# Selective scan: the last block of the convolution moved from the front into four steps of the scan

## The chip, the cores and the metric

The kernel runs on one core of a Trainium2 chip. Its time is device time in microseconds (us), the median of several executions of the whole program. The engines are PE (matrix multiply), DVE (vector), ACT (activation functions), POOL (the second elementwise engine) and SP, which here only issues transfers. Each engine works through its own list of instructions in order and waits on semaphores for the others.

## The reference, cut to what matters

Eight images of 64 x 64 positions and 96 channels go through four layers. Layers 0 and 2 are selective scans over 192 inner channels and a state of 16; layer 1 is a chunked scan, layer 3 a spectral layer. Cut to a selective scan:

```python
xm, z = split(einsum('bhwc,ec->bhwe', x, in_proj_w))
xc = silu(depthwise_conv3x3(xm) + conv_b)          # this change is about this line
xs = [xc by rows, xc by columns, both reversed]    # four directions
dts, Bs, Cs = split(x_proj_weight @ xs)
delta = softplus(dt_projs @ dts + bias)
h = h * exp(delta * A) + (delta * u) * B           # a scan over 4096 positions
y = sum over the state of h * C, plus u * D
```

The four directions are then added, normalised, gated by `silu(z)` and projected back. Everything is in float32.

## The kernel before

One image is worked on at a time, layer after layer, so there are 16 selective scans in the program (8 images, layers 0 and 2). `project` leaves the projected input in `y` (96 partitions, two halves of 192 channels, 4096 positions). `selective_scan` makes the convolution with its silu from `y` into `u`, and then runs 32 steps: four directions `k` of eight chunks of 512 positions.

**The front.** The 64 rows are cut into eight blocks of eight rows (512 positions). `conv` makes blocks 0 to 4 on DVE, tap by tap (lines 254 and 256). `conv_block` makes blocks 5, 6 and 7 on PE: nine taps for each half, each a matmul (line 267) of `y`, shifted, with a diagonal matrix of that tap's weights, summed in PSUM. The 18 diagonals are made by POOL (`diagonals`, line 261) into a buffer of the tile `c`. `silu` (line 270) on ACT adds the bias and writes `u`. Between these calls the inputs of steps 0 and 1 are prepared by `prepare_part`. PSUM buffers of the front (`p_conv`) are given back before the two buffers `da` of the steps are taken; DVE's memsets of `da` (line 674) are thus the first thing that waits for the front's last silu.

**A step** has six groups `n` of 32 channels and four states of each partition row. For each group:

- `spread` (line 541, PE) copies a group's `du` over the 128 partitions into the PSUM tile `pu`, which has one buffer.
- `with_b` (line 547) multiplies by B into `db`: on DVE, reading `pu`, for groups 0, 1, 3 and 4; on POOL for groups 2 and 5.
- `decays` (line 562, ACT) makes the exponentials into `da[0]` and `da[1]`, two instructions each.
- `scan` (line 577, DVE) runs twice, once per `da`, into `h`, of which there are five buffers.
- `leave` copies the last state (line 593, ACT) and multiplies `h` by C in place (line 598, POOL). `enter` (line 533, ACT) puts states into the `db` of a later group.
- `total_y` (lines 605 and 615, PE) sums three groups into `py`, which ACT copies to `y` (line 702). `py`, the two `pv` of `prepare` and nothing else share one PSUM buffer (the tag `py` of the pool `p_y`).

The order of all this is written out by hand: a loop over `t = 6 * i + n` (step `i`, group `n`) emits the calls, and each engine runs its instructions in the order of emission. At `n` = 2 the calls are, in order: first half scan of the group, exponentials ahead, second half scan, `leave`, `enter`, exponentials ahead, `with_b` of the next group. At `n` = 3 follow `spread` of group 4 and `total_y` of the first half. `prepare` makes the inputs of later steps in seven parts; its softplus (line 488) needs another activation table than the exponentials, so ACT loads a table before and after it. Block 7 of `u` is first read by the preparation of step 7, in step 5.

Of the kernel before, what the change touches and what calls it, by code (L numbers as in the profile page):

```python
# [9 lines left out]
F32 = mybir.dt.float32  # L10
AF = mybir.ActivationFunctionType
# [6 lines left out]
DM = 96  # L18
# [4 lines left out]
LC = 512  # L23
# [12 lines left out]
C_CW = C_OUT + 192  # L36
C_CB = C_CW + 18
# [27 lines left out]
def tile_vision_stack(  # L65
# [19 lines left out]
    nc = tc.nc  # L85
# [21 lines left out]
    ident = cst[:, K_ID : K_ID + 128]  # L107
# [34 lines left out]
    with (  # L142
# [6 lines left out]
        for i, (dtw, dtx, w) in enumerate(((dt0, dx0, w0s), (dt2, dx2, w2s))):  # L149
# [10 lines left out]
            for k in range(K):  # L160
                pw = pp.tile([DM, 2, 192], F32, name="pw", bufs=2)
                for hf in range(2):
# [4 lines left out]
                        start=True,  # L167
                        stop=True,
# [68 lines left out]
    def taps(y, rows, hf, acc):  # L237

        at, end = rows
        av = acc.rearrange("p (r c) -> p r c", c=64)  # L240
        xv = y[:, hf, :].rearrange("p (r c) -> p r c", c=64)
        for tap in (4, 0, 1, 2, 3, 5, 6, 7, 8):
            dy, dx = tap // 3 - 1, tap % 3 - 1
            r0, r1 = max(at, -dy), min(end, 64 - dy)
            c0, c1 = max(0, -dx), min(64, 64 - dx)
            src = xv[:, r0 + dy : r1 + dy, c0 + dx : c1 + dx]
            yield tap, src, av[:, r0 - at : r1 - at, c0:c1]

    def conv(w, y, u, rows, hf):
        out = u[:, hf, rows[0] * 64 : rows[1] * 64]  # L250
        for tap, src, dst in taps(y, rows, hf, out):
            cw = w[:, C_CW + hf * 9 + tap : C_CW + hf * 9 + tap + 1]
            if tap == 4:
                nc.vector.tensor_scalar_mul(dst, src, cw)
            else:
                nc.vector.scalar_tensor_tensor(dst, src, cw, dst, ALU.mult, ALU.add)
        silu(w, u, rows, hf, out)
# [7 lines left out]
    def conv_pe(dg, y, j, hf, acc):  # L265
        for tap, src, dst in taps(y, (8 * j, 8 * j + 8), hf, acc):
            nc.tensor.matmul(dst, dg[:, 9 * hf + tap, :], src, start=(tap == 4), stop=(tap == 8))

    def silu(w, u, rows, hf, acc):
        nc.scalar.activation(  # L270
            u[:, hf, rows[0] * 64 : rows[1] * 64],
            acc,
            AF.Silu,
            bias=w[:, C_CB + hf : C_CB + hf + 1],
        )
# [119 lines left out]
    def view(t, wh, at, n):  # L395

        if not wh:
            return t[:, at : at + n]
        return t.rearrange("p (h w) -> p w h", w=64)[:, at // 64 : (at + n) // 64, :]

    def cut(t, wh):

        return t.rearrange("p (w h) -> p w h", h=64) if wh else t

    def selective_scan(w, wdt, a, d, u, y):
# [23 lines left out]
        with (  # L429
# [86 lines left out]
            def groups(t):  # L516

                return t[:, 1:].rearrange("p (g s) -> p g s", s=SEG)[:, :, :LC]
# [67 lines left out]
            def leave(t, more):  # L586
# [10 lines left out]
                    prepare_part(i + 1)  # L597
                nc.gpsimd.tensor_mul(h, h, made[i]["c"])  # L598

            def total_y(i, hf):  # L600

                k, c = steps[i]
                wh = k % 2 == 1
                py = pyp.tile([128, LC], F32, name="py", tag="py")[:DM]
                nc.tensor.matmul(  # L605
                    py,
                    skip[:, hf, :] if k == 0 else ident[:DM, :DM],
                    view((u if k == 0 else y)[:, hf, :], wh, c * LC, LC),
                    start=True,
                    stop=False,  # L610
                )
                hs = [groups(made[i].pop(("h", 3 * hf + q))) for q in range(3)]
                for g in range(NSG):
                    for q in range(3):
                        nc.tensor.matmul(  # L615
                            py[32 * q : 32 * q + 32, :],
                            red,
                            hs[q][:, g, :],
                            start=False,
                            stop=(g == NSG - 1),  # L620
                        )
                return view(y[:, hf, :], wh, c * LC, LC), cut(py, wh)
# [3 lines left out]
            def prepare_part(i):  # L626
                if i < len(steps):
                    if i not in going:
                        going[i] = prepare(i)
                    next(going[i], None)  # L630
# [9 lines left out]
            with tc.tile_pool(name="p_conv", bufs=2, space=PSUM) as pvp:  # L640

                def conv_block(n):
                    acc = pvp.tile([DM, 2, LC], F32, name="acc")
                    for hf in range(2):
                        conv_pe(dg, y, n, hf, acc[:, hf, :])
                    return n, acc

                def silu_block(n, acc):
                    for hf in range(2):
                        silu(w, u, (8 * n, 8 * n + 8), hf, acc[:, hf, :])  # L650

                for hf in range(2):
                    conv(w, y, u, (0, 8), hf)
                for _ in range(5):
                    prepare_part(0)
                blocks = [conv_block(5)]
                conv(w, y, u, (8, 24), 0)
                for _ in range(2):
                    prepare_part(0)
                conv(w, y, u, (8, 24), 1)  # L660
                for _ in range(2):
                    prepare_part(1)
                blocks.append(conv_block(6))
                silu_block(*blocks[0])
                conv(w, y, u, (24, 40), 0)
                blocks.append(conv_block(7))
                silu_block(*blocks[1])
                conv(w, y, u, (24, 40), 1)
                silu_block(*blocks[2])
            with tc.tile_pool(name="p_da", bufs=1, space=PSUM) as pap:  # L670
                das = [pap.tile([128, 2 * SEG + 1], F32, name=f"da{p}") for p in range(2)]
                for da in das:
                    for at in range(3):
                        nc.vector.memset(da[:, at * SEG : at * SEG + 1], 0.0)
                states = {}
                for t in range(3):
                    enter(t)
                spread(0)
                decays(0, 0)
                decays(0, 1)  # L680
                with_b(0)
                for t in range(total + 2):
                    n, i = t % units, t // units
                    ahead = t + 1 < total
                    if n in (0, 3) and ahead:
                        spread(t + 1)
                    elif n in (1, 4) and t + 2 < total:
                        spread(t + 2)
                    if n == 0 and i > 0:
                        sums = total_y(i - 1, 1)  # L690
                    elif n == 3:
                        sums = total_y(i, 0)
                    elif n == 4:
                        prepare_part(i + 2)
                    if t < total:
                        scan(t, 0)
                        if n % 3 == 0 and t + 2 < total:
                            with_b(t + 2)
                    if ahead:
                        decays(t + 1, 0)  # L700
                    if n % 3 == 1 and t > 1:
                        nc.scalar.copy(*sums)
                    elif n == 0:
                        prepare_part(i + 1)
                    elif n == 5:
                        prepare_part(i + 2)
                    if t < total:
                        scan(t, 1)
                        leave(t, n == 3)
                    if t + 3 < total:  # L710
                        enter(t + 3)
                    if ahead:
                        decays(t + 1, 1)
                        if (n + 1) % 3 != 2:
                            with_b(t + 1)
                    if n in (0, 1, 5):
                        prepare_part(i + 1)

    def chunked_scan(w, d, u, y):

# [476 lines left out]
    for b in range(batch):  # L1197
        xd = xp.tile([DM, L], F32, name="xd")
        layers = (
            (w0s, lambda u, y: selective_scan(w0s, wdts[0], a0s, dsum[0], u, y)),  # L1200
            (w1s, lambda u, y: chunked_scan(w1s, dsum[1], u, y)),
            (w2s, lambda u, y: selective_scan(w2s, wdts[1], a2s, dsum[2], u, y)),
        )
        with tc.tile_pool(name="layers", bufs=1) as uyp:
            u = uyp.tile([DM, 2, L], F32, name="u")
            y = uyp.tile([DM, 2, L], F32, name="y")
            stats = uyp.tile([DM, 8, 6], F32, name="stats")
            sbs = [uyp.tile([DM, 2], F32, name=f"sb{n}") for n in range(3)] + [sb3]
            for n in range(4):
                with (  # L1210
# [3 lines left out]
                    if n == 0:  # L1214
                        xs = rp.tile([DM, L], F32, name="xs")
                        with (
# [3 lines left out]
                            src = x[b : b + 1].rearrange("b h w c -> (b h w) c")  # L1220
                            src = src.rearrange("(t p) c -> p t c", p=128)
# [21 lines left out]
        dst = out[b : b + 1].rearrange("b h w c -> (b h) w c").rearrange("h w c -> w h c")  # L1243
# [148 lines left out]
```

## Time and profile before

| | us |
|---|---|
| median of 3 runs | 29505.22 (29502.27 to 29553.22) |
| profiled execution, its own time | 29541.08 |
| its span | 29539.3 |
| DVE busy | 24797.7 (84%) |
| PE busy | 23139.1 (78%) |
| POOL busy | 21775.2 (74%) |
| ACT busy | 16410.5 (56%) |

Times in the trace count from the start of the span. An instruction's line gives its start, its length, its engine, its source line, the tile that it writes and those that it reads, and in brackets how long its engine had been idle before it and what ended that. The groups of the page give the number of instructions, their busy time in us and the mean length in ns, then the idle time ahead of them. A row of busy time by stretch gives the stretch, its length, the busy time of PE, PE's weight loads, DVE, ACT and POOL with the number of instructions, then PE's granted clock (1.00 is full speed), the share of the transfer engines and GB/s.

### The profile page before, as it was taken

The numbers are of one execution on the slowest core, as the hardware profiler recorded it, in microseconds if no ns is written. First come the engines' busy times: TensorE is split into PE (matmuls) and PEld (weight loads), VectorE is DVE, ScalarE is ACT, GpSimd is POOL, SyncE is SP. The second block draws the span as 40 slices with busy tenths as digits, with TensorE's granted clock in tenths as the row PEclk, the third lists the DMA queues.
The fourth block names the chain that finished last, engine by engine and source line by source line (L and its number), as shares of the span: only waits on it lengthen the run. The fifth ranks groups of instructions, "written<-read, shape, count | busy, mean of one in ns | idle before, by whom it ended". The sixth has DMA issues, their size and how long they took to land. (4 is left out here: it accounts for less than half of the span.)

```text
span 29539.3 us, 279023 instructions
## 1 busy us (share of the span) xinstructions
PE 23139.1 (78%) x89862; PEld 8801.1 (30%) x89862; DVE 24797.7 (84%) x17920; ACT 16410.5 (56%) x28541; POOL 21775.2 (74%) x8844
## 2 busy tenths in 40 slices
PE   7797877978779787797877978779787797877978
PEld 1151411514115142151421514215141151412414
DVE  9979699796897968979689796897979979699796
ACT  5546455464554645546455464554655546455564
POOL 8859488594885958859588495884958859587594
PEclk7787777877778777787777877778777787777877
DMA  5415254152541525415254152541525415254152
GB/s 124 103 38 133 66 122 102 39 133 65 121 103 39 132 67 120 104 39 131 67 118 105 38 132 68 118 105 38 132 68 122 102 38 132 67 122 102 43 131 65
DMA packets 1509730, 2727.51 MB, mean 92 GB/s; under 512 B 306584, under 2 KB 314104, under 8 KB 1503664
## 3 DMA queue, kind: packets, MB, share of 16 engines
q1 hardware_dynamic: 1491632, 2703.38, 39.2%
q8 instruction: 720, 11.80, 0.2%
q10 hardware_dynamic: 16640, 6.29, 0.1%
q14 instruction: 738, 6.05, 0.1%
HBM read 2325.26 MB, written 383.45 MB: 92 GB/s over the span
## 5 line engine op out<-in xcount | busy, mean ns | idle before, releaser
L577 DVE TENSOR_TENSOR_SCAN h<-da,db 128x1026 f32<-128x1026 f32 x6144 | 13728.7, 2280 | 505.4 <-PE py L615 170.7
L598 POOL TENSOR_TENSOR h<-h,c 128x2048 f32<-128x2048 f32 x3072 | 12749.2, 4178 | 143.2 <-ACT state L593 140.8
L541 PE MATMUL pu<-du,cst 32*128 32x512 f32 x4096 | 3238.8, 881 | 3528.1 <-DVE db L547 3493.8
L562 ACT ACTIVATE da<-dx,a0s 128x512 f32<-128x512 f32 x6144 | 4235.0, 690 | 2593.9 <-DVE h L577 2431.0
L562 ACT ACTIVATE da<-dx,a2s 128x512 f32<-128x512 f32 x6144 | 4234.9, 690 | 2593.2 <-DVE h L577 2428.1
L615 PE MATMUL py<-h,cst 128*32 128x512 f32 x24576 | 5404.1, 810 | 66.4 <-POOL h L598 66.4
L547 POOL TENSOR_TENSOR db<-du,b 128x2048 f32<-128x2048 f32 x1024 | 4653.5, 4544 | 583.9 <-ACT db L533 583.9
L547 DVE TENSOR_TENSOR db<-pu,b 128x2048 f32<-128x2048 f32 x2048 | 4637.5, 2264 | 6.7 <-issue 6.7
L615 PEld LDWEIGHTS py<-h,cst 128*32 128x32 f32 x24576 | 1177.9, 144 | 4956.0 <-issue 4505.2
L541 PEld LDWEIGHTS pu<-du,cst 32*128 32x128 f32 x4096 | 801.6, 243 | 5545.6 <-DVE db L547 4001.4
L463 PE MATMUL pv<-u,wk 96*128 96x512 f32 x2048 | 1766.6, 1004 | 751.1 <-ACT raw L459 751.1
L227 POOL TENSOR_SCALAR xn<-xs,sb 96x512 f32<-96x512 f32 x192 | 217.1, 1136 | 2773.4 <-DVE sb L207 2642.4
L454 PE MATMUL pv<-u,wk 96*96 96x512 f32 x2048 | 1486.2, 855 | 522.0 <-ACT state L593 252.1
L605 PE MATMUL py<-y,cst 96*96 96x512 f32 x1536 | 1551.3, 1108 | 400.5 <-ACT raw L468 361.6
L960 ACT ACTIVATE sg<-sg 128x768 f32<-128x768 f32 x1024 | 819.4, 800 | 1407.4 <-PE sg L944 1407.4
L506 POOL TENSOR_TENSOR du<-raw,u 96x512 f32<-96x512 f32 x1024 | 1443.9, 1434 | 0.0
L992 DVE TENSOR_TENSOR wt<-wt,cbm 128x768 f32<-128x768 f32 x1024 | 1022.3, 1004 | 496.6 <-ACT wt L961 496.4
L593 ACT COPY state<-h 128x4 f32<-128x4 f32 x3072 | 604.5, 197 | 1164.6 <-DVE h L577 1164.6
L1154 DVE SCALAR_TENSOR_TENSOR f<-p,w3bs,f 128x512 f32<-128x512 f32 x768 | 576.4, 750 | 719.6 <-ACT f L1147 692.8
L914 POOL TENSOR_TENSOR ce<-ec,cr 96x512 f32<-96x512 f32 x256 | 406.5, 1588 | 975.5 <-ACT ec L912 971.1
L891 POOL TENSOR_TENSOR rr<-lr,cc 128x768 f32<-128x768 f32 x256 | 375.9, 1468 | 1001.6 <-ACT lr L889 822.8
L463 PEld LDWEIGHTS pv<-u,wk 96*128 96x128 f32 x2048 | 534.3, 289 | 1910.2 <-ACT raw L459 1435.1
(207 smaller groups left out, 31983.9 us busy)
## 6 DMA issues: line engine op xcount, KB each, us to landing
dx<-dd SPq DMA_DIRECT2D x4096, 192.0 KB
b<-bcd SPq DMA_DIRECT2D x2048, 256.0 KB
c<-bcd SPq DMA_DIRECT2D x2048, 256.0 KB
du<-dud SPq DMA_DIRECT2D x2048, 128.0 KB
dd<-raw SPq DMA_DIRECT2D x1024, 192.0 KB
dud<-du SPq DMA_DIRECT2D x512, 128.0 KB
xd<-xs SPq DMA_DIRECT2D x256, 192.0 KB
xs<-xd SPq DMA_DIRECT2D x128, 384.0 KB
```

The source lines that it names most:

```text
L454: nc.tensor.matmul(pv[:DM], weights[k][:, hi, 128:], uv[hi], start=(hi == 0), stop=(hi == 1))
L463: nc.tensor.matmul(pv, weights[k][:, hi, :128], uv[hi], start=(hi == 0), stop=(hi == 1))
L506: nc.gpsimd.tensor_mul(cut(du[:, hf, :], wh), cut(delta[hf], wh), uv[hf])
L541: nc.tensor.matmul(pu, sel[rows, :], m["du"][rows, n // 3, :], start=True, stop=True)
L547: (nc.gpsimd if pool else nc.vector).tensor_mul(groups(m["db", n]), (m["du2"][:, n // 3, :] if pool else m["pu"]) .unsqueeze(1) .to_broadc ...
L562: nc.scalar.activation(dst[:, g, :LC], made[i]["dx"][n // 3][:, n % 3, :], AF.Exp, scale=av4[:, k, n, gs : gs + 1],)
L577: nc.vector.tensor_tensor_scan(made[i]["h", n][:, at][:, way], das[p][:, rev : 2 * SEG + rev][:, way], made[i]["db", n][:, at][:, way], 0. ...
L598: nc.gpsimd.tensor_mul(h, h, made[i]["c"])
L605: nc.tensor.matmul(py, skip[:, hf, :] if k == 0 else ident[:DM, :DM], view((u if k == 0 else y)[:, hf, :], wh, c * LC, LC), start=True, st ...
L615: nc.tensor.matmul(py[32 * q : 32 * q + 32, :], red, hs[q][:, g, :], start=False, stop=(g == NSG - 1),)
L960: nc.scalar.activation(sg, sg, AF.Abs)
L992: nc.vector.tensor_mul(it["wt"], it["wt"], m["cbm"][:, j : j + 1, :].to_broadcast([128, RK, Q]),)
```

## The change

Blocks 5 and 6 stay in the front. Block 7 is taken out of it, matmuls and silus, and made in four pieces, one at the end of group 2 of each of steps 1 to 4: half 0 in the first two, half 1 in the other two. The first piece of a half makes taps 4, 0, 1, 2 and 3; ACT copies the sum from PSUM to `u`. The second piece brings that back into PSUM with an identity matmul and adds taps 5 to 8. The diagonals are made anew for each piece by ACT, from the identity, with the tap's weight as the scale. After the fourth piece both halves get their silu in place. The accumulator takes the shared PSUM buffer `py`.

```diff
+            def conv_piece(n, piece):
+                hf, second = piece // 2, piece % 2 == 1
+                acc = pyp.tile([128, LC], F32, name="acc", tag="py")[:DM]
+                out = u[:, hf, n * LC : n * LC + LC]
+                if second:
+                    nc.tensor.matmul(acc, ident[:DM, :DM], out, start=True, stop=False)
+                mine = list(taps(y, (8 * n, 8 * n + 8), hf, acc))
+                mine = mine[5:] if second else mine[:5]
+                some = tp.tile([DM, 5, DM], F32, name="some")
+                for at, (tap, _, _) in enumerate(mine):
+                    col = C_CW + 9 * hf + tap
+                    nc.scalar.activation(
+                        some[:, at, :], ident[:DM, :DM], AF.Copy, scale=w[:, col : col + 1]
+                    )
+                for at, (tap, src, dst) in enumerate(mine):
+                    nc.tensor.matmul(
+                        dst, some[:, at, :], src,
+                        start=(tap == 4), stop=(at == len(mine) - 1),
+                    )
+                nc.scalar.copy(out, acc)
+                if piece == 3:
+                    for hf in range(2):
+                        at = slice(n * LC, n * LC + LC)
+                        nc.scalar.activation(
+                            u[:, hf, at], u[:, hf, at], AF.Silu,
+                            bias=w[:, C_CB + hf : C_CB + hf + 1],
+                        )
...
                 conv(w, y, u, (24, 40), 0)
-                blocks.append(conv_block(7))
                 silu_block(*blocks[1])
                 conv(w, y, u, (24, 40), 1)
-                silu_block(*blocks[2])
+            late = {(1 + n, 2): (7, n) for n in range(4)}
...
                     if n in (0, 1, 5):
                         prepare_part(i + 1)
+                    if (i, n) in late:
+                        conv_piece(*late[i, n])
```

More of the change, by code (lines that the diff above doesn't have):

```diff
@@ L598, in leave @@
                 nc.gpsimd.tensor_mul(h, h, made[i]["c"])
+            def conv_piece(n, piece):
[14 more added lines that the diff above has]
+                    nc.tensor.matmul(
+                        dst,
+                        some[:, at, :],
+                        src,
+                        start=(tap == 4),
+                        stop=(at == len(mine) - 1),
+                    )
[4 more added lines that the diff above has]
+                        nc.scalar.activation(
+                            u[:, hf, at],
+                            u[:, hf, at],
+                            AF.Silu,
+                            bias=w[:, C_CB + hf : C_CB + hf + 1],
+                        )
             def total_y(i, hf):
```

## The prediction

> **What bounds the kernel now.** First the page: no engine is at its peak, DVE has the most work, and the two groups that cost most belong to the selective scan, one on DVE and one on POOL.
>
> ```profile
> PE 23139.1 (78%) x89862; PEld 8801.1 (30%) x89862; DVE 24797.7 (84%) x17920; ACT 16410.5 (56%) x28541; POOL 21775.2 (74%) x8844
> ...
> L577 DVE TENSOR_TENSOR_SCAN h<-da,db 128x1026 f32<-128x1026 f32 x6144 | 13728.7, 2280 | 505.4 <-PE py L615 170.7
> L598 POOL TENSOR_TENSOR h<-h,c 128x2048 f32<-128x2048 f32 x3072 | 12749.2, 4178 | 143.2 <-ACT state L593 140.8
> ```
>
> These shares are averages over four layers, so I next asked for busy time in one stretch of one selective scan (four of its 32 steps). POOL is busy for 144.13 of 144.60 us and DVE for 141.13; a step takes 36.24 us. Both are full: a microsecond lost by DVE inside the steps is soon lost by POOL too, because each `h` has to be scanned before POOL multiplies it.
>
> ```profile
> 272.40:417.00 144.60, 107.05 (x272) 25.01 (x272) 141.13 (x65) 93.75 (x175) 144.13 (x41) 0.69 0.56 131
> ```
>
> Then the stretch ahead of the first step, engine by engine. DVE ends its share of the convolution at 103.5 us and stands still for 22.49 us. It waits for the last `silu` (L270) on ACT, and that waits for PE, which makes blocks 6 and 7 in one run of 72 passes from 92.86 (an fp32 matmul is two passes).
>
> ```profile
> 125.95 0.62 DVE L674 MEMSET da<- 128x1 f32 x6 [22.49 <-ACT u L270]
> ...
> 92.86 31.72 PE L267 MATMUL acc<-y,c 96*96 96x512 f32 x72
> ...
> 109.97 1.26 ACT L270 ACTIVATE u<-acc,w0s 96x512 f32<-96x512 f32 x2 [16.48 <-PE acc L267]
> 111.12 1.14 ACT L270 ACTIVATE u<-u,w0s 96x1024 f32<-96x1024 f32 x1
> 124.62 1.26 ACT L270 ACTIVATE u<-acc,w0s 96x512 f32<-96x512 f32 x2 [12.36 <-PE acc L267]
> 125.78 0.38 ACT L533 COPY db<-zero 128x4 f32<-128x4 f32 x3
> ```
>
> Last, the place in a step where the pieces will stand. I take step 4 and count from T0 = 290.73 us, where DVE's scans of group 2 end.
>
> ```profile
> 290.73 2.26 DVE L547 TENSOR_TENSOR db<-pu,b 128x2048 f32<-128x2048 f32 x1
> ...
> 291.05 1.41 ACT L562 ACTIVATE da<-dx,a0s 128x512 f32<-128x512 f32 x2
> 293.05 2.07 PE L541 MATMUL pu<-du,cst 32*128 32x512 f32 x2 [5.97 <-DVE db L547]
> ...
> 295.43 1.42 ACT L562 ACTIVATE da<-dx,a0s 128x512 f32<-128x512 f32 x2 [2.97 <-DVE h L577]
> ...
> 297.50 2.26 DVE L547 TENSOR_TENSOR db<-pu,b 128x2048 f32<-128x2048 f32 x1
> ...
> 299.86 4.48 DVE L577 TENSOR_TENSOR_SCAN h<-da,db 128x1026 f32<-128x1026 f32 x2
> ```
>
> PE has stood idle for 5.97 us before L541, and that matmul of two passes takes 2.07 us, where the same one at 302.48 takes 1.12. So PE is cold here. In all 16 selective scans the L541 at this place takes 2.07 us in steps 1 to 4, after 5.8 to 6.7 us of idleness.
>
> [...] Granted clock (third number from the right), with PE busy first after the length:
>
> ```profile
> 3768.85:3772.26 3.41, 0.00 (x0) 0.00 (x0) 3.34 (x3) 0.00 (x0) 3.41 (x4) 1.00 0.58 173
> 3772.26:3775.67 3.41, 2.65 (x3) 0.95 (x4) 3.23 (x4) 0.00 (x0) 3.41 (x4) 0.50 1.00 227
> 3775.67:3779.08 3.41, 3.41 (x6) 1.14 (x5) 3.34 (x4) 1.15 (x1) 3.41 (x3) 0.50 1.06 217
> 3779.08:3782.50 3.42, 3.42 (x10) 1.34 (x9) 3.35 (x3) 0.00 (x0) 3.42 (x3) 1.00 0.32 61
> ```
>
> An empty window turns PE cold; convolution taps begin at 3773.02 and PE is warm only after the first window filled from end to end, 6.06 us later. In three other dense runs it took 6.0, 5.3 and 3.7 us. [...] here the next ACTIVATE follows the 1.28 us load at once, so I use the trace.
>
> **The change part by part, per selective scan** (16 of them: 8 images, 2 layers).
>
> *Removed from the front.* 36 passes of block 7 (14.66 us from 109.92 to 124.58, all on the path) and their two silus. ACT's copies at L533, the last thing before the first exponentials, then follow the silu that ends at 112.26 instead of the one that ends at 125.88. **Gain 13.6 us.** DVE is done by then, and all transfers for step 0 have landed by about 100 us. In the 16 scans DVE's wait at L674 is 17.75 to 22.5 us, so the gain fits everywhere.
>
> *Added to steps 1 to 4.* The built program's order on DVE, POOL and SP is unchanged, and no DMA is added. ACT gets, after the L562 that ends at T0+1.73, five (or four) 96x96 activations for the diagonals [...], and then the copy of `acc`, at which it stands until PE is done. PE gets the taps between two L541: the one for group 3 and the one for group 4 that DVE needs at T0+6.77. That is the crux: L541 today ends 2.4 us ahead of its reader.
>
> - First tap: T0+1.73 and one diagonal: T0+2.1 (2.0 to 2.6). Later diagonals hide behind taps.
> - Tap cost: block 7 shows 0.84 ns per element and pass warm, twice that cold. Pieces 0 and 2 stream 2536 elements twice: 4.25 us warm. Pieces 1 and 3 stream 1834 behind the first diagonal: 3.07 us; their identity matmul runs earlier, in PE's idle time.
> - With a cold time C a piece takes its warm time + C/2. [...] So 6.8 and 5.6 us, and 0.13 for the last pass to land.
> - Pieces 0 and 2 end at T0+9.03. L541 then takes 1.0, a semaphore 0.05, and DVE's L547 for group 4 starts at T0+10.08 instead of T0+6.77: **3.3 us late**. ACT's copy (0.58) and exponentials end at T0+11.1, ahead of the scan (T0+12.4), so they cost nothing.
> - Piece 1 ends at T0+7.85: **2.1 us late**.
> - Piece 3 also has two silus with a table load on each side, as the Softplus pair has at L488 (3.94 us in all). ACT: 7.85 + 0.05 + 0.58 + 3.94 + 1.41 + 0.05 = T0+13.9 for the exponentials that the scan needs at T0+9.13: **4.75 us late**.
>
> What waits behind that: group 3's state copy on ACT and POOL's product for it move by at most 2.5 us and are caught up within the step, since DVE stays later; `py` of L615 starts later but on a warm PE, done 2 us before the scan of group 5 that reuses its `h`. DVE and POOL are both full, so next to nothing is won back; I allow 0.3 us of slack in POOL.
>
> **Sum:** 13.6 + 0.3 - (2 x 3.3 + 2.1 + 4.75 = 13.5) = 0.4 us per scan, 6 us in all. The profiled execution took 29541.08 us, 0.12% over the median 29505.22; the difference is applied to the median: **29499 us**. A measurement of this kernel can tell about 0.2% (59 us, 3.7 us per scan) from no change.
>
> **Bounds.** C = 3.4 everywhere: stalls 2 x 2.46 + 1.28 + 3.9 = 10.1, a gain of 3.8 per scan, 29444 us. Taps cold to the end (8.5 and 6.15 us): stalls 2 x 5.0 + 2.66 + 5.28 = 17.95, a loss of 4.05, 29570 us.
>
> **Rivals.**
> - *PE doesn't stay cold* (0.10, faster). If the identity matmul or an odd phase keeps the clock up, the pieces take 4.25 and 3.07 us: stalls 2 x 0.76, 0 and 2.2, a gain of 10 per scan, 29345 us. Against it: 64 of 64 cold matmuls at this place.
> - *PE never warms inside a piece* (0.14, slower). Between 294.07 and 300.90 PE is busy throughout and only the second window counted. If diagonal waits or short taps make windows that don't count, it is the cold bound: 29570. It decides from stalls above 17.6 us per scan. Against it: runs of the same taps at 3773 warmed in their first full window.
> - *The front has another limit* (0.02, slower): with no gain at L674 only the stalls are left, 16 x 13.2, 29716 us. Against it: the chain above.
> - The balance: 0.74.
>
> From these: faster 0.13 (the first rival, and 0.03 of the balance's low end); slower 0.16 (0.10 of the second rival, which lies just past the bound, the third, and 0.04 of the balance's high end); same 0.71. The range, 29440 to 29572, reaches from bound to bound; the first and third rivals stay outside it.
>
> **What would show it.** DVE's idle time at the memset (328.3 us before) falls by 218. DVE's L547 waits for PE's L541 by about 175 us in all, L577 for ACT after piece 3 by about 42 more. The granted clock is 0.5 at each first tap. I am wrong if DVE's stall per piece averages below 2.4 or above 4.3 us, or if the scan starts less than 13 us earlier.

## Result and profile after

The changed kernel takes 29523.07 us (median of 20 runs) against 29518.53 us before (20 runs). The ratio is 1.0004, with a 95% interval of 0.9997 to 1.0011. A second comparison, further down, gave 1.0011 (1.0003 to 1.0018). That is no change by the 0.2% of the forecast, which was 29499 us, no change. The second interval lies just above 1, so a loss of about 0.1% or less is more likely than the gain of 6 us that was forecast; the sign is not settled.

Nothing here was hidden: two large edits cancel. The first place to look is DVE's list of waits in the trace of after. Its columns are the waiting instruction, what it waited for, the time in all, how often, and the longest.

```profile
DVE db L547 <- PE pu L541: 175.8, 64, 6.0
...
DVE h L577 <- ACT da L562: 147.2, 311, 2.7
...
DVE da L710 <- ACT u L270: 88.3, 16, 7.8
```

The same list of before has two of these waits:

```profile
DVE da L674 <- ACT u L270: 328.3, 16, 22.5
...
DVE h L577 <- ACT da L562: 98.8, 288, 0.7
```

The memset behind the front (L710, L674 before) waits 88.3 us in 16 scans, where it was 328.3. That is the gain, 240 us. The first line of after did not exist before: DVE waits 64 times, once per piece, for PE's L541. The wait for ACT's exponentials was 98.8 us, so 48.4 us are new. The two new waits make 224 us.

The same in the page's groups of after. POOL's product L598 now waits 321.8 us (143.2 before), nearly all of it for ACT's state copy L593, and DVE's L547 waits for PE.

```profile
L598 POOL TENSOR_TENSOR h<-h,c 128x2048 f32<-128x2048 f32 x3072 | 12746.6, 4177 | 321.8 <-ACT state L593 291.1
...
L547 DVE TENSOR_TENSOR db<-pu,b 128x2048 f32<-128x2048 f32 x2048 | 4637.8, 2265 | 183.8 <-PE pu L541 175.8
```

**The front** of the first scan, in the timelines of DVE, PE and ACT:

```profile
109.78 0.62 DVE L710 MEMSET da<- 128x1 f32 x6 [6.17 <-ACT u L270]
110.86 2.29 DVE L547 TENSOR_TENSOR db<-pu,b 128x2048 f32<-128x2048 f32 x1 [0.46 <-ACT db L533]
113.78 4.48 DVE L577 TENSOR_TENSOR_SCAN h<-da,db 128x1026 f32<-128x1026 f32 x2 [0.63 <-ACT da L562]
...
92.78 15.63 PE L267 MATMUL acc<-y,c 96*96 96x512 f32 x36
...
108.45 1.26 ACT L270 ACTIVATE u<-acc,w0s 96x512 f32<-96x512 f32 x2 [14.81 <-PE acc L267]
109.60 1.14 ACT L270 ACTIVATE u<-u,w0s 96x1024 f32<-96x1024 f32 x1
110.64 0.38 ACT L533 COPY db<-zero 128x4 f32<-128x4 f32 x3
```

PE makes 36 passes (two for each of 18 matmuls) instead of 72 and DVE waits 6.17 us instead of 22.49. The memsets now run beside ACT's last silu, so the first L547 gains a little more than the front and the first scan gives 0.63 us of it back.

**A piece.** Piece 0 of the same scan, all engines:

```profile
166.02 2.27 DVE L547 TENSOR_TENSOR db<-pu,b 128x2048 f32<-128x2048 f32 x1
...
167.68 1.43 ACT L612 ACTIVATE some<-cst,w0s 96x96 f32<-96x96 f32 x5
168.10 7.93 PE L616 MATMUL acc<-y,some 96*96 96x512 f32 x10 [6.30 <-ACT some L612]
...
175.96 1.12 PE L541 MATMUL pu<-du,cst 32*128 32x512 f32 x2
176.06 0.58 ACT L623 COPY u<-acc 96x512 f32<-96x512 f32 x1 [6.96 <-PE acc L616]
...
177.12 2.29 DVE L547 TENSOR_TENSOR db<-pu,b 128x2048 f32<-128x2048 f32 x1 [4.25 <-PE pu L541]
177.16 2.51 POOL L506 TENSOR_TENSOR du<-raw,u 96x512 f32<-96x512 f32 x2 [2.07 <-PE pu L541]
```

T0 is 166.02. The taps begin at T0+2.08 after 6.30 us in which PE stood still, and ten passes take 7.93 us; L541 for group 4, in line behind them, comes at T0+9.94, and DVE's L547 at T0+11.10 where it stood at T0+6.77. Then piece 3, where ACT is the later one:

```profile
287.20 5.24 PE L616 MATMUL acc<-y,some 96*96 96x504 f32 x8 [4.89 <-ACT some L612]
287.50 4.48 DVE L577 TENSOR_TENSOR_SCAN h<-da,db 128x1026 f32<-128x1026 f32 x2
...
293.07 1.28 ACT L627 ACT_TABLE_LOAD   x1
...
293.52 2.29 DVE L547 TENSOR_TENSOR db<-pu,b 128x2048 f32<-128x2048 f32 x1 [1.55 <-PE pu L541]
...
297.02 1.41 ACT L562 ACTIVATE da<-dx,a0s 128x512 f32<-128x512 f32 x2
...
298.37 0.18 ACT L593 COPY state<-h 128x4 f32<-128x4 f32 x1
...
298.46 8.85 DVE L577 TENSOR_TENSOR_SCAN h<-da,db 128x1026 f32<-128x1026 f32 x4 [2.65 <-ACT da L562]
...
298.63 4.17 POOL L598 TENSOR_TENSOR h<-h,c 128x2048 f32<-128x2048 f32 x1 [1.94 <-ACT state L593]
```

DVE first waits 1.55 us for PE, and 2.65 us more for exponentials that stand behind two silus and two table loads of 1.28 us. POOL's wait comes from the same queue: DVE has scanned group 3 by 291.98, but the state copy that POOL's product waits for stands on ACT behind all this and starts only at 298.37.

To see the balance per scan I took from both timelines the start of every L547 on DVE; means over the 16 scans:

| us | before | after | difference |
|---|---|---|---|
| first tap of the convolution to first L547 | 82.99 | 68.11 | -14.89 |
| step 0 | 36.28 | 36.77 | +0.49 |
| step 1 (piece 0) | 36.29 | 39.64 | +3.35 |
| step 2 (piece 1) | 36.42 | 38.88 | +2.46 |
| step 3 (piece 2) | 36.59 | 39.84 | +3.24 |
| step 4 (piece 3) | 36.33 | 41.42 | +5.09 |
| steps 5 to the last L547 | | | -0.04 |
| sum | 1240.64 | 1240.35 | -0.29 |

### The profile page after: what moved, and what is told of

Its sections match the earlier page's. It is cut to its first block, busy times and chain, and to the rows that moved or that the text cites. A ratio compares the mean times of both kernels' runs of the same rounds, so it can differ in the third digit from the quotient of the medians.

```text
span 29513.6 us, 279551 instructions
## 1 busy us (share of the span) xinstructions
PE 23206.7 (79%) x89926; PEld 8831.2 (30%) x89926; DVE 24808.5 (84%) x17920; ACT 16561.3 (56%) x28925; POOL 21765.8 (74%) x8844
## 5 line engine op out<-in xcount | busy, mean ns | idle before, releaser
L577 DVE TENSOR_TENSOR_SCAN h<-da,db 128x1026 f32<-128x1026 f32 x6144 | 13728.7, 2280 | 557.0 <-PE py L649 169.7
L598 POOL TENSOR_TENSOR h<-h,c 128x2048 f32<-128x2048 f32 x3072 | 12746.6, 4177 | 321.8 <-ACT state L593 291.1
L541 PE MATMUL pu<-du,cst 32*128 32x512 f32 x4096 | 3191.8, 869 | 3119.6 <-DVE db L547 3097.8
L649 PE MATMUL py<-h,cst 128*32 128x512 f32 x24576 | 5298.5, 796 | 61.2 <-POOL h L598 61.2
L547 POOL TENSOR_TENSOR db<-du,b 128x2048 f32<-128x2048 f32 x1024 | 4656.7, 4548 | 359.1 <-ACT db L533 359.1
L547 DVE TENSOR_TENSOR db<-pu,b 128x2048 f32<-128x2048 f32 x2048 | 4637.8, 2265 | 183.8 <-PE pu L541 175.8
L541 PEld LDWEIGHTS pu<-du,cst 32*128 32x128 f32 x4096 | 791.1, 240 | 5150.1 <-DVE db L547 3514.7
L506 POOL TENSOR_TENSOR du<-raw,u 96x512 f32<-96x512 f32 x1024 | 1446.5, 1438 | 41.5 <-PE pu L541 40.9
L593 ACT COPY state<-h 128x4 f32<-128x4 f32 x3072 | 603.7, 197 | 1114.0 <-DVE h L577 1113.9
```

Source lines behind the costliest of these rows:

```text
L506: nc.gpsimd.tensor_mul(cut(du[:, hf, :], wh), cut(delta[hf], wh), uv[hf])
L541: nc.tensor.matmul(pu, sel[rows, :], m["du"][rows, n // 3, :], start=True, stop=True)
L547: (nc.gpsimd if pool else nc.vector).tensor_mul(groups(m["db", n]), (m["du2"][:, n // 3, :] if pool else m["pu"]) .unsqueeze(1) .to_broadc ...
L577: nc.vector.tensor_tensor_scan(made[i]["h", n][:, at][:, way], das[p][:, rev : 2 * SEG + rev][:, way], made[i]["db", n][:, at][:, way], 0. ...
L649: nc.tensor.matmul(py[32 * q : 32 * q + 32, :], red, hs[q][:, g, :], start=False, stop=(g == NSG - 1),)
```

## Experiments

My theory: the front gives 14.4 us per scan, and four stalls take it back, because the taps stand on PE between two matmuls of a queue that DVE waits on, and begin while PE is cold. "Cold" means that the record of PE's granted clock has 0.50 there, "warm" that it has 1.00; in the traces of before and after it has no other value (a figure between them is a mean). Rivals: both edits are worth little; the length of a piece comes from the passes and the diagonals, not from the clock; or ACT's queue is what costs. Every ratio below is to the kernel before, timed on the same chip.

### One half of the change at a time

The front's half: block 7 leaves it, and one copy stands for the pieces.

```diff
-                    if (i, n) in late:
-                        conv_piece(*late[i, n])
+                    if (i, n) == (1, 2):
+                        nc.scalar.copy(u[:, :, 7 * LC :], y[:, :, 7 * LC :])
```

> Block 7 is taken out of the front and not made in pieces: the steps copy y to u there in one ACT instruction, so the convolution, bias and silu of block 7 are left out. Balance theory: the front gives 14.6 to 14.9 us per scan and nothing takes it back, so 235 us below the kernel before (about 0.8%, ratio 0.992). Rival (block 7 was hidden anyway, the two kernels are alike because both edits are worth little): ratio above 0.998.

Measured: 29297.9 us, ratio 0.9932 (0.9919 to 0.9944), 204 us less, 31 short of what was expected. DVE's wait at the memset is 91.1 us, and no wait for PE's L541 takes its place among DVE's waits but 1.4 us:

```profile
DVE h L577 <- ACT da L562: 106.9, 302, 0.6
DVE da L710 <- ACT u L270: 91.1, 16, 7.6
...
DVE h L577 <- PE pu L541: 1.4, 2, 0.7
```

The other half: the changed kernel with block 7 in the front as well.

```diff
                 conv(w, y, u, (24, 40), 0)
+                blocks.append(conv_block(7))
                 silu_block(*blocks[1])
                 conv(w, y, u, (24, 40), 1)
+                silu_block(*blocks[2])
```

> Block 7 is made twice: in the front as before, and again in the four pieces. Balance theory: the front is as long as before and steps 1 to 4 pay their stalls of about 14 us per scan, so 225 us above the kernel before (ratio 1.0076). Rival (the pieces are hidden): ratio below 1.002.

Measured: 29766.98 us, ratio 1.0091 (1.0078 to 1.0105), 265 us more, 40 above what was expected. DVE's waits:

```profile
DVE da L712 <- ACT u L270: 296.7, 14, 22.5
DVE db L547 <- PE pu L541: 175.1, 64, 4.3
...
DVE da L712 <- ACT db L533: 38.6, 2, 20.8
```

The front's wait is back (296.7 and, put down to another ACT instruction in two scans, 38.6 make 335 us) and the pieces' wait is the same 175 us. So each edit is worth 0.7 to 0.9%, with opposite signs: the rival in which both are worth little is out.

### Is it the clock?

Six identity matmuls more fill PE's idle time ahead of the taps; the first tap overwrites their sum. (The helpers `begin`, `diags`, `pe_taps` and `finish` are the parts of `conv_piece`: take the buffer, diagonals, matmuls, copy and silus. `fill(6)` makes the six matmuls.)

```diff
                     ahead = t + 1 < total
+                    if (i, n) in late:
+                        begin()
+                        fill(6)
...
                     if (i, n) in late:
-                        conv_piece(*late[i, n])
+                        diags(*late[i, n])
+                        pe_taps(*late[i, n])
+                        finish(*late[i, n])
```

> The changed kernel with six more identity matmuls (12 passes, about 5.1 us warm) in PE's idle time at the start of group 2 of steps 1 to 4; their sum is overwritten by the first tap. Everything else keeps its order. Cold-clock theory: PE stays warm, a piece takes 4.25 or 3.1 us, DVE's wait for L541 falls from 3.4 and 2.25 us to about 0.8 and 0, the wait after the silus to about 2.2, so some 9 to 10 us per scan less: 145 to 160 us below the kernel before (ratio 0.995). Rival (the length of a piece comes from the number of passes and the waits for diagonals, not from the clock): as the changed kernel or slower, ratio 1.000 to 1.003.

Measured: 29380.41 us, ratio 0.9959 (0.9946 to 0.9971): 122 us less (145 to 160 expected), though PE has 768 passes more to do. PE's timeline around piece 0:

```profile
163.91 5.39 PE L615 MATMUL acc<-y,cst 96*96 96x512 f32 x12
169.55 4.49 PE L629 MATMUL acc<-y,some 96*96 96x512 f32 x10 [0.24 <-ACT some L608]
173.97 1.12 PE L541 MATMUL pu<-du,cst 32*128 32x512 f32 x2
```

The same ten passes take 4.49 us instead of 7.93. PE's granted clock over these taps (third number from the right), first in after, then here:

```profile
168.10:175.96 7.86, 7.86 (x11) 2.59 (x11) 4.67 (x3) 1.01 (x4) 6.99 (x2) 0.56 0.62 130
169.55:173.97 4.42, 4.42 (x10) 1.55 (x10) 4.32 (x3) 1.01 (x4) 4.42 (x2) 1.00 1.05 214
```

At the first tap the clock is 0.5 in all 64 pieces of after and 1.0 in all 64 here. DVE's waits of this kernel:

```profile
DVE h L577 <- ACT da L562: 144.2, 302, 2.6
...
DVE db L547 <- PE pu L541: 25.4, 32, 0.8
```

The wait for L541 falls from 175.8 to 25.4 us: 0.8 us behind the five-tap pieces, nothing behind the four-tap ones. The diagonals, the order and the copy are unchanged, so the clock is what made the pieces long. What is left beside these 0.8 us is the stall behind the silus.

### Is it the place?

The diagonals a step ahead, the taps at once behind the matmul for group 3.

```diff
                     ahead = t + 1 < total
+                    if (i, n) in late:
+                        begin()
+                        pe_taps(*late[i, n])
...
                     if (i, n) in late:
-                        conv_piece(*late[i, n])
+                        finish(*late[i, n])
+                    if (i + 1, n) in late:
+                        diags(*late[i + 1, n])
```

> The same pieces, with two moves: ACT makes the diagonals one step ahead (end of group 2 of steps 0 to 3), and PE runs the taps at the start of group 2, at once behind the matmul for group 3, in the idle time that is there and while the clock is still up; copy and silus stay where they are. Theory (the crux is that the taps stand between the two L541 and begin cold): taps end about 1 us after T0, before L541 for group 4 can start at T0 + 2.3; the silus end at T0 + 6.3, and the exponentials behind them at about T0 + 7.7, ahead of the scan at T0 + 9.1; no stall is left, so the whole front gain stays: 225 to 235 us below the kernel before (ratio 0.992). Rival (ACT's queue is what the pieces cost: diagonals, copy and silus): the stalls after pieces 3 remain, and the ratio is above 0.996.

Measured: 29261.96 us, ratio 0.992 (0.9905 to 0.9934), 240 us less. The timeline at piece 3, T0 = 277.09:

```profile
274.40 3.24 PE L629 MATMUL acc<-y,some 96*96 96x504 f32 x8
...
279.34 1.28 ACT L642 ACT_TABLE_LOAD   x1
279.41 1.12 PE L541 MATMUL pu<-du,cst 32*128 32x512 f32 x2 [1.78 <-DVE db L547]
...
283.29 1.42 ACT L562 ACTIVATE da<-dx,a0s 128x512 f32<-128x512 f32 x2
283.86 2.27 DVE L547 TENSOR_TENSOR db<-pu,b 128x2048 f32<-128x2048 f32 x1
...
286.23 8.85 DVE L577 TENSOR_TENSOR_SCAN h<-da,db 128x1026 f32<-128x1026 f32 x4
```

The taps end 0.55 us after T0, warm (eight passes in 3.24 us, 5.24 in after); L541 waits for its buffer, not for them; L547 and the scan stand at T0+6.77 and T0+9.14, as in the kernel before. The silus and table loads are all there, and hidden: ACT's exponentials end at T0+7.62. So ACT's queue costs only where PE makes its copy late, and that rival is out.

### The silus

Piece 3 with `AF.Exp` (scale -1, no bias) in place of `AF.Silu`: no table load stands there in this trace, where after has two of 1.28 us.

> The changed kernel with the silus of piece 3 replaced by exponentials in place, so ACT loads no table there; the silu and bias of block 7 are left out. Theory: the stall after piece 3 falls from 5.1 us to that of piece 1 (2.3 to 2.5 us), 2.6 us per scan or 42 us less than the changed kernel, ratio to the kernel before 0.9985 to 0.999. Rival (the table loads are hidden behind DVE's wait for PE): as the changed kernel, ratio 1.0004.

Measured: 29502.43 us, ratio 0.9999 (0.9991 to 1.0007). By this ratio alone it is nearer to the rival's 1.0004; beside the changed kernel on the same chip (last experiment) it is 37 us less, near the 42 of the theory, but the two intervals overlap. DVE's waits decide: the one for ACT's exponentials is 109.5 us, and that for L541 stays.

```profile
DVE db L547 <- PE pu L541: 179.4, 64, 4.7
...
DVE h L577 <- ACT da L562: 109.5, 310, 0.6
```

So the table loads, with 0.2 us per scan by which the two silus are longer than the exponentials, cost 147.2 - 109.5 = 38 us, 2.4 us per scan.

### L541 first

The taps behind the matmul for group 4 instead of ahead of it, and the copy behind that group's exponentials.

```diff
                     if n in (0, 3) and ahead:
                         spread(t + 1)
+                    if n == 3 and (i, 2) in late:
+                        begin()
+                        pe_taps(*late[i, 2])
...
                     if (i, n) in late:
-                        conv_piece(*late[i, n])
+                        diags(*late[i, n])
+                    if n == 3 and (i, 2) in late:
+                        finish(*late[i, 2])
```

> The changed kernel with the taps behind the matmul for group 4 (L541) on PE instead of ahead of it, and the copy behind the exponentials of group 4 on ACT. Theory: DVE's wait at L547 is gone, but the taps now stand ahead of the sum of the first three groups (total_y), which ends about T0 + 15 to 16.5, and the scan of group 5, at T0 + 13.5, waits for the buffer of h that it frees: the wait moves from pu to h, 1.7 to 3 us per piece, some 10 us per scan instead of 14; 60 us less than the changed kernel, ratio 0.998. Rival (only pu mattered): no stall, ratio 0.992.

Measured: 29553.32 us, ratio 1.0016 (1.0009 to 1.0022): not faster than the changed kernel. The wait moved to `h` as expected, but it is larger, and a wait for ACT that was not expected comes with it. DVE's waits:

```profile
DVE h L577 <- PE py L664: 383.9, 291, 4.1
DVE h L577 <- ACT da L562: 159.6, 280, 4.3
```

L547 waits no more, but the scan waits 213 us more for the sum on PE that frees its `h`, and 61 us more for ACT than before: 274 us, 17 per scan, where I expected 10. In step 1 of the first scan the scan of group 5 waits 3.72 us, where I had reckoned 3.0. Here, moving a cold piece along the same queue moved the wait from one reader to the next.

### Further along the same way

The early taps in steps 0 to 5: half 1 of block 6 as well, in steps 0 and 1.

```diff
-            late = {(1 + n, 2): (7, n) for n in range(4)}
+            late = {(0, 2): (6, 2), (1, 2): (6, 3, (1,))}
+            late.update({(2 + n, 2): (7, n) for n in range(4)})
```

(`conv_block` and `silu_block` leave that half out, and its first diagonals are made ahead of step 0.)

> The early taps of e4 with six pieces instead of four: half 1 of block 6 in steps 0 and 1, block 7 in steps 2 to 5, so PE's run in the front is 7.3 us shorter. Theory: the front is now set by DVE's own taps (5.5 us of DVE's wait at the memset are left in the changed kernel), so 4 to 5.5 us per scan less than e4, 60 to 90 us, ratio to the kernel before about 0.9895; the six pieces stay hidden. Rival (the pieces in steps 0 and 1, or the silus behind piece 2 of block 6, cost as much as is won): as e4, ratio 0.992 or above.

Measured: 29186.44 us, ratio 0.9895 (0.9881 to 0.9908), 319 us less than before: faster than both kernels. DVE goes from its own last tap straight to the memsets, so PE no longer bounds the front:

```profile
93.08 10.46 DVE L256 SCALAR_TENSOR_TENSOR u<-y,w0s,u 96x1008 f32<-96x1008 f32 x8
103.55 0.62 DVE L728 MEMSET da<- 128x1 f32 x6
104.84 2.29 DVE L547 TENSOR_TENSOR db<-pu,b 128x2048 f32<-128x2048 f32 x1 [0.67 <-ACT db L533]
```

These pieces also tell place and clock apart, which piece 3 of e4, early and warm, does not. In step 0 the first tap comes 7.2 us ahead of T0 and the clock there is 0.5 in all 16 scans; the ten passes take 6.4 to 8.8 us and DVE's L547 does not wait for L541. So a cold piece costs nothing here, where PE's idle time is long enough for it.

### The changed kernel again

> The changed kernel itself, for comparison on this chip: ratio 0.9997 to 1.0011 by all theories.

Measured: 29539.68 us, ratio 1.0011 (1.0003 to 1.0018).

## Why the prediction was right

Its steps, one by one, with the table's means:

- **Gain of the front**, 13.6 us: 14.89 to the first L547, less 0.49 given back in step 0, makes 14.4. Low by 0.8: the memsets had stood behind the last silu, and now run beside it.
- **First tap at T0+2.1**: T0+2.08. The time of a diagonal in it was my estimate, from no trace; in after a diagonal takes 0.36 us (L612, mean of 288), and those behind the first hide behind the taps as said.
- **Cold start of the pieces, half of the cold time added**: right, and the filler shows it as a cause. Stalls of 3.3, 2.1, 3.3 and 4.75 us, in sum 13.5, were 3.35, 2.46, 3.24 and 5.09, in sum 14.1. Pieces 1 and 3 were mis-sized by 0.3 to 0.4 us. The cold time itself, C = 5.1 us, was my estimate: I took the clock to be up again after one to two of the 3.41 us of the prediction's rows, and 5.1 as the middle. The four dense runs of before that the prediction names took 3.7 to 6.06 us, in the mean 5.3. Eight pieces of after took longer than two such stretches, 6.8 us (last section), and the prediction's own lines had a case against it: PE is busy from 293.05 and the clock is up at 300.90, 7.85 us later (it stands there under the second rival).
- **L547's wait for L541 about 175 us in all; L577's for ACT about 42 more**: 175.8 and 48.4.
- **Nothing won back**: steps 5 to the end differ by -0.04 us where I allowed 0.3 to be saved.
- **Missed**: I had POOL's queue down as unchanged but for L598. Its L506 for the next step writes the `du` that L541 reads, and so waited 40.9 us in all behind the late L541. And group 3's state copy on ACT was to move by at most 2.5 us: it starts at T0+11.88 in piece 0 and T0+13.24 in piece 3, where it stood at T0+6.88 (step 4 of before), while POOL's product for it moves by some 2 us as said. No cost of either shows in the table beyond the stalls.

The sum, 0.4 us saved per scan, was 0.29 in the profiled execution, and 0.22 lost in that of the changed kernel again. That the two edits nearly cancel was reasoned out and is what happened; that the sum is off by only 0.1 us is luck, as a gain 0.8 too low, stalls 0.6 too low and a saving of 0.3 that did not come offset each other.

The faster rival, a PE that doesn't go cold, would need idle time of PE filled, and the filler kernel is just that: it came to 29380 us where the rival stood at 29345. The slower rival, taps cold to the end, needed stalls above 17.6 us per scan; they are 14.1, and one piece of the 64 in after stays cold to its end.

What stays open is small. From the first tap of the convolution to the last L547, the 16 scans of each trace are shorter or longer than in before by -224 us (front alone), +233 (pieces alone), -145 (filler), -210 (early taps), -42 (no silus), +58 (L541 first), -315 (six pieces), and -5 and +4 (the changed kernel, twice). The measured times lie up to 39 us (0.13%) from these, on either side. Each profile is one execution, and the rest of the program, which no edit changes, takes between 9628 and 9711 us in these ten traces; so the runs do not settle where those microseconds are.

## What to carry to other kernels

Work for an idle engine is not free because the engine is idle on average: ask which instruction of its queue comes next, who waits for that, and in which clock state the work begins. The same taps cost 14 us per scan at the end of PE's idle gap, right ahead of a matmul that DVE waits on, and nothing some 5 to 6 us earlier, at the start of that gap. When two engines are full, count every stall of either at its full length, and let a balance like this one tell you that the half that gains is worth keeping and the other worth moving.

## What the hardware showed

A window is here a stretch of 3.41 us: in the traces of before and after every stretch of one granted clock, but for the last, is a whole number of these long (2346 stretches in each). In before all 368 windows at full clock in which PE does nothing are followed by one at half clock. I had estimated that the first window filled with taps brings the clock back, as the one from 3775.67 in the prediction's rows does. It doesn't always. In the first scan of after, piece 0 begins at 168.10; two windows of 3.41 us in which PE is busy throughout pass at half clock (third number from the right), and only then is it up:

```profile
168.22:171.63 3.41, 3.41 (x5) 1.16 (x6) 3.31 (x3) 0.89 (x4) 3.41 (x2) 0.50 1.03 224
171.63:175.05 3.42, 3.42 (x6) 1.17 (x5) 1.24 (x1) 0.00 (x0) 3.42 (x1) 0.50 0.37 69
175.05:178.46 3.41, 3.41 (x10) 0.82 (x11) 1.34 (x1) 2.37 (x6) 1.34 (x3) 1.00 0.00 0
```

The record of the granted clock shows how often. Of the 64 pieces of after, 56 have the clock back at the end of the first window that they fill, 3.7 to 5.7 us after the first tap. In the other eight a window begins 0.05 to 0.2 us after the first tap and passes at half clock although PE is busy throughout: seven come up at the end of the next one, after 6.9 to 7.0 us, and one stays cold to its end (8.76 us for its ten passes). In the second trace of the same kernel (the changed kernel again) this also happens to four pieces whose window begins 1.03 us after the first tap, while others with nearly the same start come up at its end. What sets a window that counts apart from one that doesn't, these runs do not show.

The stalls behind the pieces do not spread evenly either: pieces 0 and 1 cost 4.3 and 1.6 us in four scans of 16, and 2.7 to 3.4 and 2.4 to 2.5 in the other twelve. The mean cold time, 5.05 us without the piece that never came up, is close to my estimate (5.1), but that took every full window to bring the clock back and the windows to fall anywhere with equal chance. The first is not so here and the second was not shown; that part is luck.
